# Two-layer block on one core: the order in which batch 1's norm and batch 0's mixer are handed to the planner

## The chip, the core and the metric

The kernel runs on one core of one Trainium2 chip. The metric is the device time of one execution, in microseconds (us); less is better. Times are medians of several executions. Durations inside the kernel come from one profiled execution.

## The reference

The input x has 4 batches of 512 rows and 256 columns. There are two layers, each of the form x = x + s * silu(FFN(xn)), where xn is the layer norm of x. In the first layer s comes from a "mixer", a recurrence whose state starts at zero, so that it falls together into two matrix products; in the second layer s comes from attention. The FFN is gated, with a Walsh-Hadamard transform of its 1024 hidden values.

```python
# first layer, its state written out: rs = is_ = 0
xi = (xn @ W_in.T)
y = sum over 16 states of (C_real * B_real - C_imag * B_imag) * xi
s = xn + rmsnorm(y @ W_out.T, norm_w)
g = silu(fwht(silu(xn @ W1.T) * (xn @ W3.T)) @ W2.T)
x = x + s * g
# second layer
xn = layernorm(x); s = attention(xn) @ o_proj + xn
x = x + s * silu(ffn(xn))
```

All is fp32.

## The kernel before

**Numbers and products.** Each fp32 operand of a product is split into a high and a low part (`split`, L59: ScalarE rounds the high part at L61, VectorE subtracts at L62). A product is then three products: high by high, high by low, low by high (`mm3`, L80). Every matrix product and transpose goes through `matmul` (L74) or `transpose` (L77), so all TensorE work has line L70 in the profile, and one goes by the tile names.

**The first layer.** The loop at L1002 runs over the four batches b. For each it calls `ffn` (L465), which runs over 8 blocks c of 128 hidden values. Block c makes two up products of 128 x 512 (tiles `f_<b>gu`, 12 matmuls together for both halves of the gated pair), a silu on ScalarE (L526), the gate, a multiplication on VectorE (L527, "gate c" in what follows), and the split of the hidden block into `f_<b>hh` and `f_<b>hl`. The down products (`f_<b>dn`, 12 matmuls of 256 columns for a block) follow. In batch 0 they stand at the end of the code, behind all 8 blocks (`defer` is NH, L548 and L556), since W2 has yet to be transformed; the low parts of blocks 0 to 3 are subtracted late, at L543, behind gates 6 and 7 (tile `early`).

**Work beside it.** While `ffn` runs over its blocks, other work is handed in between: a list of generators, `Beside` (L881), with 16 slots, two for each block (L547 and L551). After slot k the number of finished steps has reached total * (k + 1) / 16, rounded up. In batch 0 the list is: the preparation of weights `prep_first` (L962, 12 steps: the Hadamard transform of W2 with tiles `w2b` and `w2ps`, the split of W2, the load of x1, and the mixing matrix m with tiles `wg`, `wi` and `mps`), the mixer of batch 0 (3 steps), and the norm of batch 1 (3 steps). The steps of a slot carry an edge that says that they may not be placed ahead of the latest gate on VectorE, nor ahead of the latest up product on TensorE (`after`, L462; L546 and L550).

**The two pieces that the change touches.** `norm(0, b)` (L430) first normalises x: statistics (L275, four of them, tile `ln_<b>st`), aggregates (L277), a constant added (L279), a power on GpSimd (L280, tile `ln_<b>r`), and the scaled rows `xn` (L282, four of them). Its second and third steps each transpose one half of the columns (four transposes into a PSUM bank, tile `xt_<b>tp`) and split it into `xt` (ScalarE L61, VectorE L62). The up products of batch b read `xt`. `mixer(b)` (L713) multiplies the transposed rows by the mixing matrix (tile `o`, two steps of 12 matmuls of 256 columns), copies and squares on ScalarE (L723, L725), and in its last step takes a root mean square (VectorE L727, GpSimd L728, tile `ssr`), scales (L730, tile `osb`) and adds to xn (L733). The gate of the layer for the batch (L696, L702, L704, tile `g_0g`) is handed in with the next batch and reads that sum.

**What sets the order.** The engines work their instruction queues in order. The queues are filled by a planner when the code is complete: it goes through the program with durations of its own, and on each engine places the instruction that was handed over earliest among those that are ready by its reckoning. So the order of handing is a rank and not the order of execution: a piece of late rank fills what an earlier piece leaves free. Buffers are handed out by the same plan. The PSUM banks with the tag "ms" (three of them) serve `w2ps`, `mps`, `o` and the transposes in turn. In the second layer the order of TensorE is written out by hand (L1074).

The list of batch b is put together like this:

```python
tasks.append((mixer(b), MIXER))
if b + 1 < B:
    if b:
        load_x(b + 1)
    if b == 2:
        tasks.append((prep_s(0), 4))
    tasks.append((norm(0, b + 1), NORM))
```

Of the kernel before, what the change touches and what calls it, by code (L numbers as in the profile page):

```python
# [35 lines left out]
def kernel(ctx: ExitStack, tc: tile.TileContext, a: dict, out: bass.AP):  # L36
# [7 lines left out]
    def t4(name, shape, dt=F32):  # L44
        return act.tile(shape, dt, tag="t4", name=name, bufs=10)

    def t2(name, shape, dt=F32):
        return act.tile(shape, dt, tag="t2", name=name, bufs=6)
# [4 lines left out]
    def small(name):  # L53
        return act.tile([P, NT], F32, tag="small", name=name, bufs=16)

    def psum(name, shape, tag="ms", bufs=3):
        return ps.tile(shape, F32, tag=tag, name=name, bufs=bufs)

    def split(src, hi, lo, engine=nc.vector):  # L59

        h = nc.scalar.copy(hi, src)  # L61
        return h, engine.tensor_tensor(lo, src, hi.bitcast(F32), ALU.subtract)  # L62
# [14 lines left out]
    def transpose(*args):  # L77
        return in_line(nc.tensor.transpose, *args)

    def mm3(o, terms, late=False):  # L80


        seq = [(l[0], r[0]) for l, r in terms]
        if late:
            seq += [(l[1], r[0]) for l, r in terms] + [(l[0], r[1]) for l, r in terms]
        else:
            for l, r in terms:
                seq += [(l[0], r[1]), (l[1], r[0])]
        for n, (l, r) in enumerate(seq):
            ins = matmul(o, l, r, start=n == 0, stop=n == len(seq) - 1)  # L90
        return ins
# [128 lines left out]
    def sl(i):  # L220
        return slice(i * P, (i + 1) * P)
# [32 lines left out]
    def moments(name, x, mr):  # L254

        st = act.tile([P, NT, 6], F32, tag="stats", name=f"{name}st", bufs=4)
        mv = act.tile([P, NT, 2], F32, tag="mv", name=f"{name}mv", bufs=4)
        for t in range(NT):
            nc.vector.bn_stats(st[:, t, :], x[:, t, :])
        for t in range(NT):  # L260
            nc.vector.bn_aggr(mv[:, t, :], st[:, t, :])
        nc.vector.tensor_copy(mr[:, 0, :], mv[:, :, 0])
        first["moments"] = nc.vector.tensor_scalar(mr[:, 1, :], mv[:, :, 1], LN_EPS, None, ALU.add)
        nc.gpsimd.tensor_tensor(mr[:, 1, :], mr[:, 1, :], mhalf, ALU.pow)

    def layernorm(name, x, y, groups=(NT,)):

        t0 = 0
        for i, n in enumerate(groups):
            ts_ = range(t0, t0 + n)  # L270
            st = act.tile([P, NT, 6], F32, tag="stats", name=f"{name}st{i}", bufs=4)
            mv = act.tile([P, NT, 2], F32, tag="mv", name=f"{name}mv{i}", bufs=4)
            r = small(f"{name}r{i}")
            for t in ts_:
                nc.vector.bn_stats(st[:, t, :], x[:, t, :])  # L275
            for t in ts_:
                nc.vector.bn_aggr(mv[:, t, :], st[:, t, :])  # L277
            rs = r[:, t0 : t0 + n]
            nc.vector.tensor_scalar(rs, mv[:, t0 : t0 + n, 1], LN_EPS, None, ALU.add)  # L279
            nc.gpsimd.tensor_tensor(rs, rs, mhalf[:, :n], ALU.pow)  # L280
            for t in ts_:
                ins = nc.vector.tensor_scalar(  # L282
                    y[:, t, :], x[:, t, :], mv[:, t, 0:1], r[:, t : t + 1], ALU.subtract, ALU.mult
                )
            t0 += n
        return ins

    def transpose_half(name, y, k):
        o = psum(f"{name}tp{k}", [P, S])
        for t in range(NT):  # L290
            transpose(o[:, sl(t)], y[:, t, sl(k)], ident)
        return o
# [14 lines left out]
    def xt_pair(name):  # L307

        both = act.tile([P, 2, 2, S], F32R, tag="xt", name=name, bufs=2)
        return both[:, 0], both[:, 1]  # L310
# [119 lines left out]
    def norm(layer, b):  # L430
        xn = act.tile([P, NT, D], F32, tag="xn", name=f"xn{layer}_{b}", bufs=3)
        xns[layer, b] = xn
        with after(first["gate"] if b > 1 - layer else None):
            first["scaled"] = layernorm(f"ln{layer}_{b}", xs[b], xn)
        yield
        if layer:


            mr = act.tile([P, 2, NT], F32, tag="mr", name=f"mr{b}", bufs=2)
            moments(f"ln2_{b}", xn, mr)  # L440
            yield
            o = psum(f"mrp{b}", [2 * NT, P], **DN[b == 0])
            transpose(o, mr.rearrange("p a t -> p (a t)"), ident)
            rows = act.tile([2 * NT, P], F32, tag="rows", name=f"rows{b}", bufs=1)
            with after(first["table"] if b else None):
                nc.scalar.copy(rows, o)
            there = dram.tile([2 * NT, P], F32, tag="rows", name=f"there{b}")
            nc.sync.dma_start(there, rows)
            mrb = t4(f"mrb{b}", [P, 2, S])
            nc.sync.dma_start(  # L450
                mrb, there.rearrange("(a t) p -> a (t p)", a=2).unsqueeze(0).to_broadcast([P, 2, S])
            )
            mrs[b] = mrb
            yield
            return
        hi, lo = xTs[0, b] = xt_pair(f"xt0_{b}")
        for k in range(2):
            o = transpose_half(f"xt0_{b}", xn, k)
            split(o, hi[:, k, :], lo[:, k, :])
            yield  # L460

    def after(ins):  # L462
        return tc.issue_after(ins.ins) if ins else nullcontext()
# [249 lines left out]
    def mixer(b):  # L713

        xn, xT, m = xns[0, b], xTs[0, b], first["m"]
        osb = t4(f"osb{b}", [P, NT, D])
        r = small(f"ssr{b}")
        junk = t2(f"junk{b}", [P, D])
        for i in range(2):
            o = psum(f"o0_{b}_{i}", [P, 2, D])  # L720
            for j in range(2):
                mm3(o[:, j, :], k_pairs(xT, sl(2 * i + j), m, ALLD))
            nc.scalar.copy(osb[:, 2 * i : 2 * i + 2, :], o)  # L723
            for t in (2 * i, 2 * i + 1):
                nc.scalar.activation(junk, osb[:, t, :], AF.Square, accum_out=r[:, t : t + 1])  # L725
            yield
        nc.vector.tensor_scalar(r, r, 1.0 / D, RMS_EPS, ALU.mult, ALU.add)  # L727
        nc.gpsimd.tensor_tensor(r, r, mhalf, ALU.pow)  # L728
        for t in range(NT):
            nc.vector.scalar_tensor_tensor(  # L730
                osb[:, t, :], osb[:, t, :], r[:, t : t + 1], nwb, ALU.mult, ALU.mult
            )
        nc.vector.tensor_tensor(xn, xn, osb, ALU.add)  # L733
        yield
# [178 lines left out]
    def call(f, *args):  # L913
        f(*args)
        yield


    NORM, MIXER, W2P = 3, 3, 12
# [83 lines left out]
    for b in range(B):  # L1002
        tasks = []
        if b == 0:
            prep = prep_first()
            next(prep)
            tasks.append((prep, 12))
        if b:
            tasks.append((call(gate_all, f"g0_{b - 1}", dn, xns[0, b - 1], xs[b - 1]), 1))
        tasks.append((mixer(b), MIXER))  # L1010
        if b + 1 < B:
            if b:
                load_x(b + 1)
            if b == 2:
                tasks.append((prep_s(0), 4))
            tasks.append((norm(0, b + 1), NORM))
        if b == 0:
            early = w2_tile("early0"), w2_tile("early1")
            spare = [
                [early[i][:, 2 * c : 2 * c + 2, :].rearrange("p a d -> p (a d)") for i in range(2)]  # L1020
                for c in range(NH // 2)
            ]
        if b == 1:
            raw2_1 = load_w2(1)
            w2_1 = w2_tiles(1)
            tasks.append((prep_w2(1, raw2_1, w2_1, t4), W2P))
            tasks.append((prep_second(), 5))
        if b == 2:
            tasks += [(prep_s(1), 4), (norm(1, 0), NORM), (prep_s(2), 4)]
        if b == 3:  # L1030
            atts = [Attention(0)]
            at = atts[0]
            parts = run(at.xt_half, 0), run(at.xt_half, 1), at.xt, at.scaled, at.split_sums
            tasks += [(call(f), 1) for f in parts]
            norms = {1: norm(1, 1)}
            tasks.append((prep_s(3), 4))
        bg = Beside(*tasks)
        if b == 0:
            dn = ffn("f0_0", xTs[0, 0], w13, w2, bg.slot, NH, spare, parts=2, behind=True)
        else:  # L1040
            tail = [run(atts[0].tq, j) for j in range(2)] if b + 1 == B else []
            dn = ffn(f"f0_{b}", xTs[0, b], w13, w2, bg.slot, tail=tail)
        bg.finish()
# [148 lines left out]
```

## Time and profile before

| | |
|---|---|
| median of 3 runs | 359.23 us (359.09 to 359.24) |
| the profiled execution's own time | 359.27 us |
| its span, first to last instruction | 357.5 us |
| TensorE matmul busy | 351.5 us |
| TensorE weight loads busy | 327.4 us |
| VectorE busy | 287.1 us |
| ScalarE busy | 197.6 us |
| GpSimd busy | 20.8 us |

In the profile, PE is TensorE's matmuls, PEld its weight loads, DVE VectorE, ACT ScalarE, POOL GpSimd, SP SyncE. A row of the timeline has the start and the length in us, the engine, the line, the operation, the tile written and the tiles read, the shape where one is given, and the number of instructions that were merged; in brackets stands how long the engine was idle ahead of it and what ended that. A row of the waits has who waited for whom, and then us in total, times, and the longest. TensorE's matmuls overlap: each is shown with its full length, so the distance from start to start tells more than the busy share.

### The profile page before, as it was taken

What the parts mean: (1) busy time and instruction counts of PE and PEld (TensorE: products, weight loads), DVE (VectorE), ACT (ScalarE), POOL (GpSimd) and SP (SyncE); (2) the same over time, 40 slices, a digit from 0 to 9 for tenths busy, and PEclk for the clock granted to TensorE, in tenths of its full rate; (3) what the DMA queues carried; (4) which work ended last, traced back from release to release, by engine and by line L of the source; (5) the groups of instructions that cost most, each with busy time, mean ns of one, the idle gap of its engine ahead of it and who ended that gap; (6) DMA issues with size and microseconds to landing.
All of it is one profiled execution on the core that took longest, in us unless ns stands there. A gap on an engine that the chain in (4) does not pass through costs nothing.

```text
span 357.5 us, 6272 instructions
## 1 busy us (share of the span) xinstructions
PE 351.5 (98%) x2477; PEld 327.4 (92%) x2477; DVE 287.1 (80%) x597; ACT 197.6 (55%) x373; POOL 20.8 (6%) x22
## 2 busy tenths in 40 slices
PE   8999999999999999999999999999999999999995
PEld 6878998888988898888999999999999999999995
DVE  6899648998579938898887957989679897568645
ACT  3666156256373424674367655576555676556443
POOL 2000110300020210100110001100011000000000
PEclk9999999999999999999999999999999999999999
DMA  7935000301044416656357145562554745345401
GB/s 222 357 95 202 2 1 2 92 25 61 0 151 160 163 27 219 256 177 198 129 208 254 27 191 207 205 224 105 205 193 150 230 169 205 142 150 192 194 2 59
DMA packets 16284, 52.25 MB, mean 146 GB/s; under 512 B 1632, under 2 KB 7936, under 8 KB 16256
## 3 DMA queue, kind: packets, MB, share of 16 engines
q1 hardware_dynamic: 15968, 51.60, 41.0%
q8 instruction: 19, 0.31, 0.4%
q10 hardware_dynamic: 288, 0.26, 0.2%
q14 instruction: 9, 0.07, 0.1%
HBM read 42.40 MB, written 9.45 MB: 145 GB/s over the span
## 4 chain that ended last, share of the span: by engine, by line
PE 98%; DVE 1%; ACT 0%; issue 0%; DVEq 0%
PE f_1dn L70 6%; PE f_2dn L70 6%; PE f_1gu L70 6%; PE f_0dn L70 6%; PE f_0gu L70 6%; PE f_2gu L70 6%; PE f_3gu L70 6%; PE f_3dn L70 6%; PE sc L70 4%; PE pv L70 4%; PE o L70 3%; PE v L70 3%; PE tq L70 3%; PE warm L70 2%; PE w2ps L70 1%; PE pt L70 1%
## 5 line engine op out<-in xcount | busy, mean ns | idle before, releaser
L70 PE MATMUL f_1gu<-xt,w 128*128 128x512 f32 x96 | 24.9, 396 | 0.3 <-ACT xt L61 0.3
L70 PE MATMUL f_3gu<-xt,w 128*128 128x512 f32 x96 | 25.0, 396 | 0.0
L70 PE MATMUL f_2gu<-xt,w 128*128 128x512 f32 x96 | 24.8, 395 | 0.0
L70 PE MATMUL f_0gu<-xt,w 128*128 128x512 f32 (+1 forms) x108 | 24.4, 379 | 0.0
L70 PEld LDWEIGHTS f_0gu<-xt,w 128*128 128x128 f32 x108 | 18.5, 188 | 4.5 <-issue 1.0
L70 PEld LDWEIGHTS f_1gu<-xt,w 128*128 128x128 f32 x96 | 17.0, 188 | 3.6 <-ACT xt L61 0.5
L70 PEld LDWEIGHTS f_2gu<-xt,w 128*128 128x128 f32 x96 | 17.0, 188 | 3.0
L70 PEld LDWEIGHTS f_3gu<-xt,w 128*128 128x128 f32 x96 | 17.0, 188 | 2.9
L61 ACT CAST f_2hh<-f_2h 128x512 fp32r<-128x512 f32 x16 | 10.0, 622 | 15.3 <-DVE f_2h L527 12.2
L70 PE MATMUL f_3dn<-w2l,f_3hh 128*128 128x256 f32 x64 | 17.7, 281 | 0.0
L70 PE MATMUL f_1dn<-w2l,f_1hh 128*128 128x256 f32 x64 | 17.7, 281 | 0.0
L70 PE MATMUL f_3dn<-w2h,f_3hh 128*128 128x256 f32 x64 | 17.7, 281 | 0.0
L70 PE MATMUL f_2dn<-w2h,f_2hh 128*128 128x256 f32 x64 | 17.7, 282 | 0.0
L70 PE MATMUL f_1dn<-w2h,f_1hh 128*128 128x256 f32 x64 | 17.6, 280 | 0.0
L70 PE MATMUL f_2dn<-w2l,f_2hh 128*128 128x256 f32 x64 | 17.6, 280 | 0.0
L70 PE MATMUL f_3dn<-w2h,f_3hl 128*128 128x256 f32 x64 | 17.0, 281 | 0.0
L70 PE MATMUL f_1dn<-w2h,f_1hl 128*128 128x256 f32 x64 | 17.0, 281 | 0.0
L70 PE MATMUL f_2dn<-w2h,f_2hl 128*128 128x256 f32 x64 | 16.7, 281 | 0.0
L61 ACT CAST f_3hh<-f_3h 128x512 fp32r<-128x512 f32 (+1 forms) x17 | 10.0, 594 | 10.2 <-DVE f_3h L527 6.0
L61 ACT CAST f_1hh<-f_1h 128x512 fp32r<-128x512 f32 x16 | 9.9, 622 | 9.7 <-DVE f_1h L527 6.6
L62 DVE TENSOR_TENSOR f_2hl<-f_2h,f_2hh 128x512 fp32r<-128x512 f32 x16 | 11.0, 686 | 4.5 <-ACT f_2hh L61 4.5
L62 DVE TENSOR_TENSOR f_3hl<-f_3h,f_3hh 128x512 fp32r<-128x512 f32 (+1 forms) x17 | 11.1, 655 | 3.7 <-ACT f_3hh L61 3.6
(487 smaller groups left out, 1149.0 us busy)
## 6 DMA issues: line engine op xcount, KB each, us to landing
sw<-s SPq DMA_DIRECT2D x32, 896.0 KB, 5.3
s<-sp SPq DMA_DIRECT2D x8, 512.0 KB, 4.6
s<-sp SPq DMA_DIRECT2D x8, 384.0 KB, 2.8
w2raw<-in_w SPq DMA_DIRECT2D x4, 512.0 KB, 5.4
sraw<-in_w SPq DMA_DIRECT2D x4, 512.0 KB, 3.3
mrb<-there SPq DMA_DIRECT2D x4, 512.0 KB, 3.7
w13raw<-in_w SPq DMA_DIRECT2D x3, 512.0 KB, 6.8
x<-in_x SPq DMA_DIRECT2D x3, 512.0 KB, 3.6
```

Source lines behind the costliest of these rows:

```text
L61: h = nc.scalar.copy(hi, src)
L62: return h, engine.tensor_tensor(lo, src, hi.bitcast(F32), ALU.subtract)
L70: ins = call(*args, **kwargs)
```

## The change

In batch 0 alone the norm of batch 1 comes ahead of the mixer of batch 0 in the list. In the other batches the order stays. No instruction is added, removed or altered.

```diff
-        tasks.append((mixer(b), MIXER))
+        if b:
+            tasks.append((mixer(b), MIXER))
         if b + 1 < B:
             if b:
                 load_x(b + 1)
             if b == 2:
                 tasks.append((prep_s(0), 4))
             tasks.append((norm(0, b + 1), NORM))
+        if b == 0:
+            tasks.append((mixer(b), MIXER))
```

## The prediction

> **What bounds the kernel now.** I read the page first, then the waits, then TensorE start by start around the point where the first layer passes from batch 0 to batch 1. The page:
>
> ```profile
> PE 351.5 (98%) x2477; PEld 327.4 (92%) x2477; DVE 287.1 (80%) x597; ACT 197.6 (55%) x373; POOL 20.8 (6%) x22
> ...
> PE 98%; DVE 1%; ACT 0%; issue 0%; DVEq 0%
> ```
>
> TensorE is busy all along, and the chain that ended last is TensorE's. Reordering removes no matmul, so all it can save is time in which TensorE stands. All the waits of TensorE:
>
> ```profile
> PE warm L70 <- DVE zr L929: 1.4, 1, 1.4
> PE f_1gu L70 <- ACT xt L61: 0.3, 1, 0.3
> ```
>
> The first lies at the start, ahead of anything changed. The second is the boundary: batch 1's first up product (f_1gu) waits for the cast of batch 1's transposed norm (xt). The timeline of TensorE there:
>
> ```profile
> 50.66 0.38 PE L70 MATMUL xt_1tp<-ident,xn 128*128 128x128 f32 x2
> 50.80 0.36 PE L70 MATMUL f_0dn<-w2l,f_0hh 128*128 128x256 f32 x1
> 51.00 0.28 PE L70 MATMUL f_0dn<-w2h,f_0hl 128*128 128x256 f32 x1
> 51.60 0.73 PE L70 MATMUL f_1gu<-xt,w 128*128 128x512 f32 x2 [0.33 <-ACT xt L61]
> ```
>
> Batch 1's transposes are among the last things TensorE does for batch 0, so their evacuation stands open. VectorE's timeline (rows between left out) shows that their input was there long before:
>
> ```profile
> 32.71 0.69 DVE L527 TENSOR_TENSOR f_0h<-f_0h,f_0gu 128x512 f32<-128x512 f32 x1
> ...
> 34.51 1.41 DVE L275 BATCH_NORM_STATS2 ln_1st<-x 128x6 f32<-128x256 f32 x4
> ...
> 41.58 1.39 DVE L282 TENSOR_SCALAR xn<-x,ln_1mv,ln_1r 128x256 f32<-128x256 f32 x4 [1.12 <-POOL ln_1r L280]
> ```
>
> The norm begins once the gate of block 6 (32.71) is out, and xn is whole at 42.97, but the transposes run from 49.63 to 50.8: 6.7 us later, because TensorE works its queue in the order that was planned.
>
> **What the Trainium skill says.** "Perfetto Trace Analysis", section Identifying the Most-Contended Engine: TensorE's matmul busy share is no measure of its headroom, since matmuls are pipelined; one takes LDWEIGHTS busy instead and looks for the gaps in its regime. The trace agrees: the page has 0.33 us of matmul idle at the boundary, but the weight loads have 0.53 there, and from start to start it is 0.60 (51.00 to 51.60) where a 256-column product otherwise follows in 0.118. So I measure the hole by starts. The same page, Sequencer Loop: an engine instruction waits in its queue for its semaphore; that fits transposes which sit in order behind f_0dn while their data is ready. No other page bears on this change: all its operations have rows in the trace.
>
> **The change, part by part.** Nothing is added or removed: the same 13 VectorE, 1 GpSimd, 8 TensorE and 2+2 evacuation instructions of norm(0, 1), and the same 24 matmuls and evacuations of mixer(0), change places in the hand-over. Neither issues a DMA; x1 was loaded from 21.39 and landed about 3.0 us later (the row of x), so SyncE's queue is not passed by anything. On GpSimd each has one pow of 1.01 us, and norm's already comes first (40.54 against 48.41).
>
> Places: b = 0 has 12 + 3 + 3 = 18 steps in 16 slots, slot k brings the count to 18(k+1)/16 rounded up. Steps 13 to 15 fall in slots 10, 11, 12; steps 16 to 18 in slots 13, 14, 15. Before, the mixer has the first three and the norm the last; after, the other way round. So norm's VectorE part may start behind gate 5 (28.20 + 0.69 = 28.9) and no more behind gate 6 (33.4), and it outranks gates 6 and 7, their subtractions, and the mixer.
>
> (1) VectorE, norm earlier. It is 1.41 (stats) + 0.5 (aggregates) + 0.18 + 1.39 (xn) = 3.5 us, with 1.1 us of waiting for the pow. VectorE has no idle time from 20 to 40.4 us, so it shifts rather than shrinks. What stands behind it in before's order up to xn, and may now come after it, is hl6, gate 7, two late subtractions and hl7: about 0.6 + 0.6 + 1.2 + 0.6 = 3.0 us; gate 6 and its two late subtractions are another 1.8. I take xn whole 3 to 5 us earlier, at 38 to 40. Cover: VectorE is idle 5.19 us from 42.97 anyway, and TensorE holds 24 products of the mixing matrix, w2ps and 96 down products (11.3 us at 0.118) to fill with. The last subtraction, hl7, would end up to 3 us after 40.4, at 43.4; TensorE uses block 7's products in its last 1.4 us (12 x 0.118) ahead of 51. Cost: nothing; without that cover up to 3.5 us.
>
> (2) TensorE, transposes earlier. They follow xn in the plan, so they move about as many us ahead of 49.6, to 44.6 to 46.6. Eight take 0.91 us either way (four groups of 0.34 less one 0.118 product in each). Then two casts (1.07) and two subtractions (1.28) come in by about 49.5, ahead of 51.1. The hole closes: 0.60 - 0.118 = 0.48 us ahead of the first f_1gu, and the second, which waits for the second cast, starts 0.34 after the first where 0.233 is usual: 0.11. Sum 0.59 us. What is late next? Nothing that I find: batch 1 uses the up weights that are already there, and its first banks come free with gates 6 and 7, by about 40. The next two boundaries are this case already: batch 2's transposes ran at 72.8 to 74.0 and f_2gu began at 88.4 without a wait.
>
> (3) Mixer later. Its 24 products take 2.8 us wherever they lie. They shared the three "ms" banks with the transposes before and still do; now the transposes take two first, until VectorE has subtracted. I let o end 1 to 2 us later than 45.85. Behind it hang squares, ssr, pow, osb (1.67), xn add (1.23) and the gate of batch 0 (1.28 + 1.29): 5.5 us of VectorE, ending at 55.98. In their midst stand the xt subtractions, 1.28 us that now come earlier, so the chain would end at 54.7 and VectorE is idle until 57. So 2 us of delay costs nothing; bounds 0 and 1.5 us (rival D).
>
> (4) All later orders are planned anew. TensorE has no wait there in before. But 27 or so starts after 60 us come 80 to 110 ns later than their kind's pace (318 for 233 at 74.03), 2.5 us in all; a new order can win or lose a few of them. I take 0, bounds -0.4 and +0.3.
>
> Sum: the profiled execution took 359.27 us (span 357.5 and 1.8 around it); 359.27 - 0.59 = 358.68. The median of the runs shown is 359.23, 0.04 lower: 358.6.
>
> **The rivals.** *A: as worked out,* 358.6, its own range 358.4 to 358.8: 52 in 100. It lies so near the bound of 358.51 that I split it 23 to 29.
>
> *B: the hole closes and more comes.* With xt there from about 49.5, f_1gu can also fill under the last down products, VectorE gets batch 1's first gate sooner (it idles 0.99 us at 56), and some of the late starts of (4) go: 359.23 - 0.59 - 0.4 = 358.2. For it: these are the only losses on TensorE. Against: nobody waits for that gate. 17 in 100.
>
> *C: the wait is only exchanged,* or the plan leaves the transposes where they are, because VectorE's dependent steps of the norm are each let past by other work (stats at 34.51, aggregates only at 38.81), or because the mixer's first product keeps a bank. Then 359.2: 11 in 100. It speaks against it that 2 us of advance suffice.
>
> *D: slower, by the mixer's late chain.* From 57 to 80 us VectorE is busy 22.94 of 23.00 (the windows view), so what doesn't end by 57 pushes all behind it. If the banks, or the rank, push o to the end of batch 0 (51.1 instead of 45.85, 5.25 later), the chain ends at 54.7 + 5.25 = 59.95, 2.95 past 57. Batch 1's own chain then has xn(2) at 71.2 against its transposes at 72.76, 1.5 us in hand, so TensorE stands 1.45: 359.23 - 0.59 + 1.45 = 360.1. It turns the gain into a loss from 57 + 1.5 + 0.59 - 54.7 = 4.4 us of delay, that is o later than about 50.2. Against it: down products rank behind the mixer. 20 in 100, 2 of which within the bound.
>
> **How the numbers follow.** What a measurement of this kernel can tell from no change is about 0.2%, 0.72 us: faster is under 358.51, slower over 359.95. Faster: 23 of A and 17 of B, 0.40. Same: 29 of A, 11 of C, 2 of D, 0.42. Slower: 18 of D, 0.18. For 8 in 10 the range takes A, C, nearly all of B, and D as far as 360.1: 358.1 to 360.1. Cases of one sign hold most of it.
>
> **What would show it.** In the changed profile: no wait of f_1gu for xt among TensorE's waits; stats of ln_1 at 29 to 33 us, xn whole by 40; transposes of xt_1 no later than 47, with f_0dn following them, and f_1gu following the last product in 0.12 us (A); f_1gu ahead of the last f_0dn (B); transposes still behind 49 and a wait of the same size (C); o ending past 50.2, VectorE without idle time at 56, and a wait of TensorE between 57 and 80 (D). I am wrong altogether if TensorE waits for a gate or a late subtraction between 33 and 50 us, or if the difference comes from the second layer.

## The result and the profile after

| | before | changed |
|---|---|---|
| median (six runs of each) | 359.20 us | 360.89 us |
| lowest to highest | 359.09 to 359.24 | 360.60 to 361.34 |
| profiled execution, its span | 359.27, 357.5 us | 360.84, 359.1 us |

The ratio is 1.0048, with a 95% interval of 1.0037 to 1.0058: slower by 1.7 us. The forecast was 358.6 us, and its range ended at 360.1.

The gain that was forecast is there. TensorE's timeline in the changed kernel, at the boundary from batch 0 to batch 1:

```profile
51.03 0.28 PE L70 MATMUL f_0dn<-w2l,f_0hh 128*128 128x256 f32 x1
51.15 0.28 PE L70 MATMUL f_0dn<-w2h,f_0hl 128*128 128x256 f32 x1
51.27 1.09 PE L70 MATMUL f_1gu<-xt,w 128*128 128x512 f32 x4
```

The first up product of batch 1 starts 0.12 us after the last down product, and the next three follow it at their pace. The hole of 0.59 us is closed. But all of TensorE's waits in the changed kernel are these:

```profile
PE warm L70 <- DVE zr L929: 1.5, 1, 1.5
PE f_3dn L70 <- DVE f_3hl L62: 0.6, 1, 0.6
PE f_2dn L70 <- DVE f_2hl L62: 0.5, 1, 0.5
```

The wait for xt is gone, and two others have come, for low parts of the hidden blocks in batches 2 and 3, 60 and 120 us behind the change. TensorE's timeline shows the later one from start to start, 170.75 to 171.64, 0.89 us where 0.118 is usual:

```profile
170.75 0.28 PE L70 MATMUL f_3dn<-w2l,f_3hh 128*128 128x256 f32 x1
171.64 0.39 PE L70 MATMUL f_3dn<-w2h,f_3hl 128*128 128x256 f32 x1 [0.61 <-DVE f_3hl L62]
```

Since a matmul's shown end is modelled, I sum TensorE's standing by starts: what a start-to-start distance has over the pace of the matmul ahead of it (0.233 us for 512 columns, 0.174 for 384, 0.118 for 256, 0.109 for a 128-column transpose), where that is over 0.06 us, counted at the start of the matmul ahead. In us, by stretch of the span:

| kernel | 0-30 | 30-50.5 | 50.5-60 | 60-80 | 80-105 | 105-122 | 122-160 | 160-178 | from 178 | sum | span |
|---|---|---|---|---|---|---|---|---|---|---|---|
| before | 3.90 | 0.26 | 0.68 | 0.17 | 0 | 0.17 | 0.25 | 0 | 1.59 | 7.01 | 357.5 |
| changed | 4.03 | 0.45 | 0 | 0.49 | 0 | 0.91 | 0.25 | 0.88 | 1.66 | 8.68 | 359.1 |

The sums differ by 1.67, the spans by 1.6: this is the whole loss. It is -0.68 at the boundary, +0.19 and +0.32 up to 80 us, +0.74 near 114 and +0.88 near 171, and the rest is small. Each of the four pairs of transposes stands 0.09 us over the pace; one of them counted at the boundary before and counts before 50.5 now. So the hole itself gave 0.59, and 0.10 us came at 39.5, ahead of a product that reads `early`. Up to 30 us, ahead of all that changed, the profiles of these kernels, run 7 apart, differ by up to 0.6 us (3.66 to 4.27), so a sum is read stretch by stretch.

**Near 71.** The mixer's second half comes late. The order of TensorE's queue shows why it could: the transposes took two of the three shared banks, then the first half of o the third, and the second half stands behind 23 down products of lower rank, at 47.76 to 49.2 us (before, o had ended at 45.85). From the changed kernel's chain of work (start, length, what):

```profile
45.04 2.72 PE f_0dn L70 x23
47.76 1.44 PE o L70 x12
```

VectorE's timeline, first a row of the kernel before:

```profile
48.16 0.17 DVE L727 TENSOR_SCALAR ssr<-ssr 128x4 f32<-128x4 f32 x1 [5.19 <-ACT junk L725]
```

and then of the changed one, with rows left out:

```profile
39.81 1.37 DVE L282 TENSOR_SCALAR xn<-x,ln_1mv,ln_1r 128x256 f32<-128x256 f32 x4
...
50.92 0.17 DVE L727 TENSOR_SCALAR ssr<-ssr 128x4 f32<-128x4 f32 x1 [5.13 <-ACT junk L725]
...
59.28 0.68 DVE L704 TENSOR_TENSOR x<-x,g_0g 128x512 f32<-128x512 f32 x1
...
70.86 0.67 DVE L62 TENSOR_TENSOR f_1hl<-f_1h,f_1hh 128x512 fp32r<-128x512 f32 x1
```

The root mean square comes at 50.92 instead of 48.16, the mixer's chain ends at 59.96 instead of 55.98, and the low part f_1hl is done at 71.5, when TensorE has been at its door since 71.37. The waits do not name this one: by the modelled ends it is no wait.

**Near 114.** ScalarE's timeline, first of the kernel before:

```profile
108.53 0.62 ACT L61 CAST f_2hh<-f_2h 128x512 fp32r<-128x512 f32 x1 [2.64 <-DVE f_2h L527]
109.06 0.59 ACT L526 ACTIVATE f_2h<-f_2gu 128x512 f32<-128x512 f32 x1
110.90 0.83 ACT L61 CAST sp<-sraw 128x768 fp32r<-128x768 f32 x1 [1.25 <-DMA sraw<-in_w]
```

and then of the changed one:

```profile
109.37 0.84 ACT L61 CAST sp<-sraw 128x768 fp32r<-128x768 f32 x1 [4.18 <-DMA sraw<-in_w]
110.11 0.61 ACT L61 CAST f_2hh<-f_2h 128x512 fp32r<-128x512 f32 x1
110.63 0.59 ACT L526 ACTIVATE f_2h<-f_2gu 128x512 f32<-128x512 f32 x1
```

Two casts have changed places. `sp` belongs to the preparation of the second layer's weights (`prep_s`, L325) and waits for a load. Put ahead of `f_2hh`, it keeps that one waiting for a load that it doesn't need: the gate was out at 108.2, and the cast came at 110.11. "PSUM — Partial Sum Buffer" of the Trainium skill, section Engine vs sequencer instructions, has it that ScalarE's and VectorE's queues are strictly first in, first out; the trace agrees, since `f_2hh` stood for 1.9 us, 1.15 of them beside an idle ScalarE.

But that delay alone is not what TensorE waited for. `f_2hh` was done at 110.7, and its low part `f_2hl` began only at 113.71, with VectorE busy all the time between. With the casts their subtractions (L62) have changed places on VectorE too. First the kernel before, then the changed one, rows left out:

```profile
112.32 0.66 DVE L62 TENSOR_TENSOR f_2hl<-f_2h,f_2hh 128x512 fp32r<-128x512 f32 x1
...
114.46 0.93 DVE L62 TENSOR_TENSOR sp<-sraw,sp 128x768 fp32r<-128x768 f32 x1
```

```profile
112.71 0.93 DVE L62 TENSOR_TENSOR sp<-sraw,sp 128x768 fp32r<-128x768 f32 x1
...
113.71 0.66 DVE L62 TENSOR_TENSOR f_2hl<-f_2h,f_2hh 128x512 fp32r<-128x512 f32 x1
```

So TensorE waited for `f_2hl` because `sp`'s subtraction stood ahead of it: begun at 112.71 instead, `f_2hl` would have been done by 113.4, an estimate from these rows, and TensorE was there at 113.8. The runs below move cast and subtraction together and don't part them.

**Near 171.** SyncE's timeline, first of the kernel before, then of the changed one:

```profile
148.78 0.32 SPq L353 DMA_DIRECT2D sw<-s  x1
149.15 0.42 SPq L328 DMA_DIRECT2D sraw<-in_w  x1
156.68 0.32 SPq L353 DMA_DIRECT2D sw<-s  x1
```

```profile
149.40 9.18 SPq L353 DMA_DIRECT2D sw<-s  x2
158.67 0.38 SPq L328 DMA_DIRECT2D sraw<-in_w  x1
```

Here two loads have changed places. The second layer's weights (`sw`, L353) wait for a buffer that one of batch 3's last up products leaves at 158.24. The last raw weights (`sraw`, L328) now stand behind that wait, and go out 9.5 us later. VectorE shows the rest: it idles for the load, does its work later, and `f_3hl` comes behind that. Its timeline of the kernel before, and then of the changed one, rows left out:

```profile
164.44 1.23 DVE L62 TENSOR_TENSOR sp<-ssum,sp 128x1024 fp32r<-128x1024 f32 x1 [0.26 <-ACT sp L61]
...
168.80 0.66 DVE L62 TENSOR_TENSOR f_3hl<-f_3h,f_3hh 128x512 fp32r<-128x512 f32 x1
```

```profile
164.31 0.42 DVE L333 TENSOR_TENSOR ssum<-sraw 128x256 f32<-128x256 f32 x1 [1.68 <-DMA sraw<-in_w]
...
169.05 1.20 DVE L62 TENSOR_TENSOR sp<-ssum,sp 128x1024 fp32r<-128x1024 f32 x1
170.17 0.68 DVE L62 TENSOR_TENSOR tql<-tq,tqh 128x512 fp32r<-128x512 f32 x1
...
170.93 0.66 DVE L62 TENSOR_TENSOR f_3hl<-f_3h,f_3hh 128x512 fp32r<-128x512 f32 x1
```

### The profile page after: what moved, and what is told of

Same layout as the page of the kernel before. It is cut to its first block, busy times and chain, and to the rows that moved or that the text cites. A ratio compares the mean times of both kernels' runs of the same rounds, so it can differ in the third digit from the quotient of the medians.

```text
span 359.1 us, 6272 instructions
## 1 busy us (share of the span) xinstructions
PE 352.2 (98%) x2477; PEld 327.6 (91%) x2477; DVE 286.6 (80%) x597; ACT 197.5 (55%) x373; POOL 18.9 (5%) x22
## 4 chain that ended last, share of the span: by engine, by line
PE 84%; DVE 10%; DMA 2%; ACT 1%; issue 1%; POOL 0%; DVEq 0%; SPq 0%
PE f_0gu L70 6%; PE f_0dn L70 6%; PE f_2dn L70 5%; PE f_1dn L70 5%; PE f_3dn L70 5%; PE f_3gu L70 5%; PE sc L70 4%; PE pv L70 4%; PE v L70 3%; PE f_2gu L70 3%; PE o L70 2%; PE f_1gu L70 2%; PE tq L70 2%; PE warm L70 2%; DMA sraw<-in_w 2%
## 5 line engine op out<-in xcount | busy, mean ns | idle before, releaser
L62 DVE TENSOR_TENSOR f_2hl<-f_2h,f_2hh 128x512 fp32r<-128x512 f32 x16 | 10.9, 682 | 3.8 <-ACT f_2hh L61 3.7
L62 DVE TENSOR_TENSOR f_3hl<-f_3h,f_3hh 128x512 fp32r<-128x512 f32 (+1 forms) x17 | 11.0, 654 | 3.4 <-ACT f_3hh L61 3.3
```

## The experiments

Theory 1: three places in which a queue was filled in another order, each with its own standing. Theory 2: the mixer is late once, and the later waits follow from that. Theory 3: scatter of a new plan. An edge in what follows says that an instruction may not be placed ahead of another on its queue; it adds no work. In the code, `first` keeps an instruction under a name, `after` sets the edge, and `GU` stands for the PSUM banks of the up products. Lines that are not shown are marked by "...".

**1. The changed kernel, with the load's old place.**

```diff
-        nc.sync.dma_start(raw, a["w13_1"][q])
+        first["sraw"] = nc.sync.dma_start(raw, a["w13_1"][q])
...
-            nc.sync.dma_start(parts[i].bitcast(F32), sdram[q][i])
+            with after(first["sraw"] if n == 1 else None):
+                nc.sync.dma_start(parts[i].bitcast(F32), sdram[q][i])
```

> The changed kernel (360.89 us), with one edge more: the first weight load of the second layer's second group (sw) may not be placed ahead of the last load of raw weights (sraw) on SyncE's queue, as it stood in the kernel before. Theory 1 (three separate places in which an in-order queue was filled in another order, each with its own standing of TensorE: 0.33 us at 71, 0.74 at 114, 0.88 at 171): the last wait goes, 360.0 us, and TensorE waits for f_2hl alone, not for f_3hl. Theory 2 (the mixer of batch 0 is late and makes VectorE late once, and the later waits follow from that): 360.9, f_3hl is still waited for. Theory 3 (no cause but a new plan's scatter): anything within 0.5 us of 360.9.

Measured: 359.87 us, beside 359.25 for the kernel before; ratio 1.0016 (1.0009 to 1.0022). TensorE's waits in its profile:

```profile
PE f_2dn L70 <- DVE f_2hl L62: 0.5, 1, 0.5
PE f_0dn L70 <- DVE early L544: 0.2, 1, 0.2
```

The wait for f_3hl is gone, and 1.0 us with it; by starts the stretch from 160 to 178 has 0. One order of two loads on SyncE was worth more than the hole. The small wait for `early` (0.4 us by starts, at 38.9) is larger than in the changed kernel, which stands 0.1 there: VectorE is only just in time.

**2. The changed kernel, with the cast behind block 2's.**

```diff
-                split(h, hh, hl)
+                first.setdefault(name, []).append(split(h, hh, hl)[0])
...
-            split(src[:, :n, :], *parts)
+            with after(first["f0_2"][2] if (q, at) == (1, 0) else None):
+                split(src[:, :n, :], *parts)
```

> The changed kernel with another edge: ScalarE's first cast of the second group of raw weights (sp from sraw, which waits for a load) may not be placed ahead of the cast of block 2's hidden part in batch 2 (f_2hh), as it stood in the kernel before. In the plan made so the load order on SyncE is also that of before. Theory 1: both later waits go, 360.89 - 0.74 - 0.88 = 359.3 us, only a wait near 71 is left. Theory 2: 360.9 less at most 0.2. Theory 3: anything within 0.5 of 360.9.

Measured: 359.52 us; ratio to before 1.0009 (1.0001 to 1.0017). Both waits for low parts are gone, and the loads went back to their old order too; near 71 TensorE stands as in the changed kernel. A smaller wait came in:

```profile
PE f_2gu L70 <- DVE f_2h L528: 0.2, 1, 0.2
```

0.37 us by starts, at 114.64: an up product waits for a gate. The edge put the waiting cast behind block 2's cast but ahead of block 3's silu. That silu was done at 110.7; the gate came only at 114.41, since on VectorE `sp`'s subtraction (113.48, 0.93 us) had moved behind `f_2hl` but still stood ahead of the gate.

**3. Only the norm's rows first.** The first of the norm's three steps is handed over ahead of the mixer, the transposes behind it, on the kernel before. `step_of` takes one step from a generator.

```diff
+        ahead = norm(0, b + 1) if b == 0 else None
+        if b == 0:
+            tasks.append((step_of(ahead), 1))
         tasks.append((mixer(b), MIXER))
...
-            tasks.append((norm(0, b + 1), NORM))
+            tasks.append((ahead or norm(0, b + 1), NORM - 1 if b == 0 else NORM))
```

> The kernel before, with only the first of the norm's three steps (VectorE's statistics and scaled rows) handed ahead of the mixer, the transposes behind it. In its order all 24 products of the mixer stand at 36 to 41 us of TensorE's work (39 to 44 in the kernel before, 41 to 47 in the changed one), the transposes at 42, and both exchanges of queue places (ScalarE's cast, SyncE's load) are as in the changed kernel. Theory 1: the hole at 51 is closed (-0.59), no wait at 71, both later ones stay (+0.74, +0.88): 359.2 + 1.0 = 360.2 us. Theory 2: with the mixer early VectorE is in time and nothing is left to wait for: 358.6.

Measured: 360.13 us; ratio 1.0024 (1.0014 to 1.0034). The waits:

```profile
PE f_3dn L70 <- DVE f_3hl L62: 0.6, 1, 0.6
PE f_2dn L70 <- DVE f_2hl L62: 0.2, 1, 0.2
```

By starts there are 0 from 50.5 to 60, 0.17 from 60 to 80 as in the kernel before, 0.66 near 114 and 0.85 near 171. The mixer is early, nothing waits at 71, and both later waits are there all the same. Theory 2 falls.

**4. The same with both edges** (those of 1 and 2).

> The kernel of the run with the rows first, with both edges (cast behind f_2hh, weight load behind the raw load). Theory 1: hole closed, no wait of TensorE left but the one at the start, 359.2 - 0.59 = 358.6 us, faster than both kernels. Theory 2: the same as the run with the rows first alone.

Measured: 358.91 us; ratio 0.9990 (0.9982 to 0.9999). The two edges take 1.2 us off. 0.3 us more than expected; by starts they lie near 114 again (0.48), for the reason found in 2.

**5. The same, with the cast one place further,** which is where the kernel before has it.

```diff
             first["silu"] = nc.scalar.activation(h, gu[0], AF.Silu)
+            first.setdefault(name, []).append(first["silu"])
...
-            split(src[:, :n, :], *parts)
+            with after(first["f0_2"][3] if (q, at) == (1, 0) else None):
+                split(src[:, :n, :], *parts)
```

> The kernel with the rows first and the load edge, its cast edge put one instruction further: the cast of the raw weights may not be placed ahead of block 3's silu in batch 2, the very place it has in the kernel before. In the run with both edges that silu stood behind the waiting cast, and TensorE stood 0.2 us at 114.6 for the gate behind it. Theory 1: that goes too, 358.9 - 0.2 = 358.7 us (the hole's 0.59 less than before, 358.65). If the order of the cast is not what holds the gate up: 358.9 again.

Measured: 358.76 us; ratio 0.9988 (0.9982 to 0.9995). By starts 0.17 is left from 105 to 122. TensorE has one wait left, that at the start (1.5 us). On VectorE the gate (112.73) now stands ahead of `sp`'s subtraction (113.46).

**6. The changed kernel with the same two edges** (load as in 1, cast as in 5).

> The changed kernel with the same two edges as the rows-first kernel of this call. All that is left of the change's loss is then the mixer's late second half (its products at 46 to 47 us of TensorE's work instead of 38 to 41). Theory 1: TensorE stands 0.33 us at 71 behind a late subtraction, so 0.3 to 0.5 us more than the rows-first kernel: 359.1 us. If the lateness of the mixer costs nothing by itself: 358.7 as there.

Measured: 359.14 us; ratio 0.9999 (0.9991 to 1.0007). The edges alone give back the whole loss, 360.89 to 359.14, and the kernel stands where it stood before: the closed hole has been spent. By starts 0.49 lie from 60 to 80 (0.17 in run 5) and 0.45 from 30 to 50.5 (0.26). The 0.32 at 71 are the price of the mixer's lateness; of the other 0.19, 0.10 stand at 39, where VectorE is busier in batch 0, and the rest is the pace of one more pair of transposes.

Theory 3 named no place. Each edge took away the wait that it was aimed at, and runs 1 to 6 lie within 0.31 us of what Theory 1 had said; scatter is no explanation of that.

**7. The transposes in other banks.** As 6, and:

```diff
-        o = psum(f"{name}tp{k}", [P, S])
+        o = psum(f"{name}tp{k}", [P, S], **(GU if name == "xt0_1" else {}))
```

> The changed kernel with both edges and one thing more: batch 1's transposes go to the banks of the up products instead of the three that the mixer uses. In its order the mixer's second half stands at 39 to 40.5 us of TensorE's work and no more at 46. If the late second half comes from the banks that the transposes hold, and makes the wait at 71: no wait there, 358.7 us; a wait between 30 and 50 for an up bank may cost 0 to 0.6 of that. If the wait at 71 has another cause: it stays, 359.1.

Measured: 365.26 us; ratio 1.0174 (1.0160 to 1.0188). The waits of TensorE:

```profile
PE mps L70 <- DVE wil L62: 2.0, 1, 2.0
...
PE mps L70 <- ACT wih L61: 1.1, 1, 1.1
PE w2ps L70 <- DVE w2bl L62: 0.8, 1, 0.8
```

This answers little. The transposes took banks from batch 0's last up products, the mixing matrix's products moved up in the queue, and TensorE waited for their operands. By starts the profiled execution (366.28 us) stands 7.1 us more than run 6 before 50.5. Not all of it is waiting: TensorE was busy for 3.13 of the 7 us from 26 to 33, and from 33 to 38 the granted clock was 0.50 (1.00 in run 6), with 256-column products 0.21 us apart instead of 0.118. There is no wait at 71, but with all of this before it that proves nothing.

**8. The exchange of the loads alone, on the kernel before:** the load edge turned round.

```diff
+            ins = nc.sync.dma_start(parts[i].bitcast(F32), sdram[q][i])
+            if n == 1 and i == 0:
+                tc.add_manual_dep(first["sraw"].ins, ins.ins.name, ...)
```

> The kernel before with nothing changed but one place on SyncE: the last load of raw weights is put behind the first weight load of the second layer's second group, which waits for a buffer; in the changed kernel these two are exchanged. Theory 1: the exchange alone costs what it cost there, 0.88 us less what VectorE had in hand: 359.8 to 360.1 us, with a wait of TensorE at 170 for f_3hl. Theory 2 (a consequence of VectorE's lateness, harmless in the kernel before): 359.25.

Measured: 359.44 us beside 359.18; ratio 1.0008 (1.0001 to 1.0014). By starts TensorE stands 0.27 from 160 to 178, for f_3hl: the exchange costs by itself, so Theory 2 fails here too, but a third of what it cost in the changed kernel, and my figure was wrong. VectorE's timeline of this run:

```profile
168.65 1.21 DVE L62 TENSOR_TENSOR sp<-ssum,sp 128x1024 fp32r<-128x1024 f32 x1
169.78 0.24 DVE L277 BATCH_NORM_AGGREGATE ln_1mv<-ln_1st 128x2 f32<-128x6 f32 x2
169.93 0.66 DVE L62 TENSOR_TENSOR f_3hl<-f_3h,f_3hh 128x512 fp32r<-128x512 f32 x1
```

In the changed kernel a subtraction of the attention (`tql`, 170.17, 0.6 us) stands between `sp` and `f_3hl`, and the load went out 1.35 us later (158.67, here 157.32). So the 0.88 were the exchange together with what was placed around it.

**9. The mixer's second half in a bank of its own.** As 6, and:

```diff
-            o = psum(f"o0_{b}_{i}", [P, 2, D])
+            o = psum(f"o0_{b}_{i}", [P, 2, D], **(GU if (b, i) == (0, 1) else {}))
```

> The changed kernel with both edges, and with one tile moved: the mixer's second product of batch 0 takes a bank of the up products (free by then) instead of one of the three that it shares with batch 1's transposes. In its order these 12 products stand at 36 to 39 us of TensorE's work instead of 46 to 47; the transposes stay where they are, at 42. If the bank made the second half late and that made the wait at 71 (Theory 1): no wait there, and 0.3 to 0.4 us less than with the edges alone (359.14): 358.75. If the wait at 71 comes from the norm's earlier work on VectorE: it stays, 359.1.

Measured: 358.64 us beside 359.18; ratio 0.9986 (0.9980 to 0.9993). That is 0.5 us less than run 6. By starts: 0.35, 0, 0.17 and 0 in the four stretches from 30 to 105. The root mean square comes at 48.83 and the windows view shows VectorE with room again, 14.73 of 15.00 us busy from 57 to 72. A row of that view has the stretch, its length, and the busy time of PE, PEld, DVE, ACT and POOL with their counts; then the granted clock and the DMA's share and rate:

```profile
57.00:72.00 15.00, 15.00 (x84) 12.89 (x83) 14.73 (x32) 6.79 (x15) 2.38 (x2) 1.00 0.22 71
```

where run 6 has no room left and TensorE loses 0.06 by the modelled ends:

```profile
57.00:72.00 15.00, 14.94 (x80) 12.51 (x79) 15.00 (x33) 5.63 (x14) 2.15 (x2) 1.00 0.15 43
```

The mixer's products end at 45.8, in run 6 at 48.9. The banks made the second half late, and its lateness made the wait at 71. With the three costs taken away, the change that lost 1.7 us gains 0.5. This is the fastest version found, with run 5 0.12 us behind it, within the scatter of both.

## Why the prediction was wrong

**What bounds the kernel: right.** TensorE's order, with one hole of 0.59 us; it closed by that amount.

**(1) VectorE, norm earlier: the price held nearly, the size didn't.** Statistics began at 28.84, in the place forecast, but xn was whole at 41.2 and not at 38 to 40: the steps of the norm each let other work past (statistics 28.84, aggregates 31.74 to 33.8, the sum at 36.74). The cost was taken at nothing; it was 0.10 us at 39.5, ahead of a product that reads a late low part.

**(2) Transposes earlier: right in effect, wrong in the reckoning.** I let them move by as much as xn. They moved by 7.1 us (49.63 to 42.55) while xn moved 1.8: the place in a queue does not shift in proportion with its input.

**(3) Mixer later: the mechanism was right, the size was off.** I named the three banks, and took 1 to 2 us of delay at no cost. o ended 3.3 us later (49.2) and TensorE stood 0.32 more at 71. Rival D priced 5.25 us of delay at 1.45 and set its point at 50.2. It costs earlier, since other work of batch 1 (a gate, one pair of W2 steps, a low part) was put in between the mixer's last steps and drew the chain out to 59.96.

**(4) Later orders: this is the step that failed.** "I take 0, bounds -0.4 and +0.3." It was +1.62: 0.74 and 0.88. The late starts that I had in view were not it: by the table's measure they hold 2.2 us in the kernel before (25 starts, not "27 or so" and 2.5) and about as much in the changed one. I had argued from the trace before, in which TensorE has no wait there. But a queue without a wait may have one place between it and a wait. The casts `f_2hh` and `sp` stood 2.4 us apart on ScalarE, their subtractions 2.1 us apart on VectorE, the loads 7.5 us apart on SyncE, and nothing but the plan held them in that order. "SyncE's queue is not passed by anything" was true of the moved pieces and false of the queue. Of the 1.69 us of loss, runs 1, 2 and 6 put 1.75 on these two places; run 9 puts 0.5 on the banks; and the gain is 0.59; together 1.66.

**The rivals.** D had the sign and a real part of the loss, not its bulk. The range ended at 360.1 because (4) was given 0.3. D's point of 50.2 was not reached, o ended at 49.2, and TensorE stood at 71 all the same. The last sign named, a difference that comes from the second layer, came in good part: `sraw`, `sp` and `sw` prepare its weights. One reading of the lines was off without harm: x1 landed 3.6 us after 21.39, not 3.0.

**Open.** Why the planner made both exchanges was not settled, and no run holds the cast late without its subtraction. All the kernels here whose rows were handed over first had both exchanges, unless an edge forbade them, with the mixer early or late; the kernel before and run 8 kept the cast in place. In run 2 the loads followed the cast. That fits a near tie by the planner's clock which the earlier batch 1 tips over; it is argued from the orders, not shown.

## What to carry to other kernels

Where a planner fills in-order queues by its own clock, a change of rank must be costed over the whole program: look for instructions that wait for a load or a buffer and stand just behind work that TensorE needs, follow what depends on them onto the other queues, and give them a fixed place before anything else is moved. A moved piece takes its buffers with it: count the banks that it holds, and who of lower rank gets ahead meanwhile. And when a small gain doesn't appear, sum the bottleneck's standing by starts, stretch by stretch: here that showed the gain intact and three losses far from the change, each of which one edge or one bank took away.

## What was not expected of the hardware

The first raw load of the second layer's weights, with no other load just ahead of it, landed in 3.3 us in the kernel before (issued at 81.79). The last one stood right behind one of the weight loads (`sw`) in both kernels and took 5.7 us before (149.15 to 154.87) and 5.5 in the changed one (158.67 to 164.19): the exchange moved its issue and not its duration.

A cast that waited for such a load left ScalarE idle for 4.18 us, and the next cast, whose input was ready after 3.0 of these, stood behind it. What TensorE waited for there was the order on the busy VectorE, as said above.

In run 7, after TensorE had been busy for 3.13 of 7 us, the granted clock stood at 0.50 for the next 5.
